# Edges of a graph network kernel laid on 128 partitions of 416 columns instead of 125 of 425

## The chip, the cores and the metric

The kernel runs on one core of one Trainium2 chip. The metric is device time in microseconds (us), the median of 16 runs. All numbers of the profile below come from one profiled execution on that core.

## The reference

A stack of four graph layers on 3,125 nodes of 256 features and 53,125 directed edges (25,000 edges both ways and one loop per node, sorted by destination `dst`). Each layer takes `h = relu(layernorm(x))` and adds its result to `x`.

```python
edge_index = jnp.stack([src, dst])
h = relu(layernorm(x)); x = x + L0(h, edge_index, edge_attr_64, ...)   # MLP message per edge, segment_sum over dst, MLP, layernorm
h = relu(layernorm(x)); x = x + L1(h, edge_index, edge_type_64, ...)   # attention, 4 heads, softmax per dst node
h = relu(layernorm(x)); x = x + L2(h, edge_attr_64, ..., edge_index)   # here dst = edge_index[0], src = edge_index[1]: sums over the SOURCE list
h = relu(layernorm(x)); x = x + L3(h, edge_index, ...)                 # attention, 1 head, then LSTM gates
```

Layer L2 reads the same edge list the other way round: it sums over what L0, L1 and L3 call the source. Its edges must therefore be sorted by source. `edge_attr_64` has 64 floats per edge.

## The kernel before, in words

Nodes are handled in 25 blocks of 128 (`NB`, `P`). Layers L0, L1 and L3 work by slots: the nodes are sorted by degree, and slot s of a block gathers the s-th neighbour of each of its 128 nodes by an indirect DMA (`gather`, line 154). L2 works by tiles: every block of 128 source nodes has 18 tiles of 128 edge records (the last block 8), 440 tiles in all.

`prelude` (line 243) sorts. It loads `dst`, `src`, `type` and the list `nxt_i` (each edge's next `dst`) as tiles of 125 partitions x 425 columns (`EP`, `EC`, lines 253 to 269): `dst_i` and the features `xh` on SyncE's queue (SP), the others on ScalarE's. It counts degrees by one-hot matmuls in two chunks of columns (`counted`, line 325: 153 VectorE comparisons and one matmul per column), ranks the nodes, and writes L0's table for the source nodes to DRAM (`table`, line 353). Between these the statistics of the layer norm are taken (`stats`, line 341). By running sums over 25 block masks (`scans`, line 461) it finds for each edge the row `row2` of the source-sorted record table `ss` in DRAM (line 555). Rows of `ss` that get no edge must read as empty: 40 DMAs fill the whole table from `sfill` before (line 304).

`by_slots` (line 561) then runs L0, L1, L2, L3. A record of `ss` is 66 floats: 64 attributes, the destination and the source's place in its block. The records are written during L0 and L1, column after column, by `scatter_src` (line 597): `loaded` (line 585) brings `CH = 5` columns of attributes of all 125 partitions into one of two buffers `rec` by a DMA on SP, `filled` (line 591) adds the two other fields by two VectorE copies, and five indirect DMAs (`scatter`, line 157) each write one column, 125 rows of 264 bytes. In L0's main loop each of 226 pairs of slots issues two gathers `gt` and, from the 19th on, one scatter. After the loop comes a drain: a hand-made clock (`Clock`, line 164) finishes the node updates, with two scatters per tick. In L1 the rest is spread over the groups of four slots, and 8 columns come at the end (line 1115).

GpSimd (POOL) issues all indirect DMAs, in the order in which they are written (`queued`, line 139). On SP and VectorE a scheduler sets the order of the instructions: it moves `loaded` and `filled` ahead of the place where they are written. An instruction of SP that waits holds up all behind it.

If a count of the input does not fit the planned slots and tiles, `flag` sends the program to another, slower path (`by_blocks`), which does not run here.

Of the kernel before, what the change touches and what calls it, by code (L numbers as in the profile page):

```python
# [9 lines left out]
F32 = mybir.dt.float32  # L10
I32 = mybir.dt.int32
BF = mybir.dt.bfloat16
AF = mybir.ActivationFunctionType
ALU = mybir.AluOpType
# [4 lines left out]
P = 128  # L19
N = 3125  # L20
NB = 25
NP = NB * P
LAST = N - (NB - 1) * P
E = 53125
EP, EC = 125, 425
# [5 lines left out]
NT = 440  # L31
# [3 lines left out]
SREC = 66  # L35
# [12 lines left out]
TILES = (18,) * (NB - 1) + (8,)  # L48
TM = TILES[0]
FR = mybir.dt.float32r  # L50
assert sum(TILES) == NT
XH = 516
# [4 lines left out]
def flat(ap, n):  # L57

    return bass.AP(tensor=ap.tensor, offset=ap.offset, ap=[[n, 1], [1, n]])


class Kit:


    last = [None, None]
# [158 lines left out]
class Lists:  # L224


    def __init__(self, pool):
        self.nid_i = pool.tile([P, NB], I32, name="nid_i")
        self.nid3_i = pool.tile([P, NB], I32, name="nid3_i")
        self.off_i = pool.tile([P, NB], I32, name="off_i")  # L230
        self.deg = pool.tile([P, NB], F32, name="deg")
        self.has = pool.tile([P, NB], F32, name="has")
        self.st = pool.tile([P, NB, SM, 2], I32, name="st")
        self.pen = pool.tile([P, NB, SM], F32, name="pen")
        self.srcb = pool.tile([P, NB, 2, HM], I32, name="srcb")
        self.ai = pool.tile([P, 2, NB], I32, name="ai")
        self.row2 = pool.tile([EP, EC], I32, name="row2")
        self.dst_e = pool.tile([EP, EC], F32, name="dst_e")
        self.srcl_e = pool.tile([EP, EC], F32, name="srcl_e")
# [3 lines left out]
def prelude(ctx, tc, a, a_d, nodes_d, ss, st_d, flag, t):  # L243
# [9 lines left out]
    dst_i = c.tile([EP, EC], I32, name="dst_i")  # L253
    nc.sync.dma_start(dst_i, a["dst"].rearrange("(p c) -> p c", c=EC))
# [5 lines left out]
    e_src = c.tile([EP, EC], I32, name="e_src")  # L260
    nc.scalar.dma_start(e_src, a["src"].rearrange("(p c) -> p c", c=EC))
    e_typ = c.tile([EP, EC], I32, name="e_typ")
    nc.scalar.dma_start(e_typ, a["edge_type_64"].rearrange("(p c) -> p c", c=EC))
    nxt_i = c.tile([EP, EC], I32, name="nxt_i")
    nc.gpsimd.memset(nxt_i, N)
    for p0, p1, w in ((0, EP - 1, EC), (EP - 1, EP, EC - 1)):
        nc.scalar.dma_start(nxt_i[p0:p1, 0:w],
                            bass.AP(tensor=a["dst"].tensor, offset=a["dst"].offset + p0 * EC + 1,
                                    ap=[[EC, p1 - p0], [1, w]]))
# [6 lines left out]
    sfill = c.tile([P, 11, SREC], F32, name="sfill")  # L276
# [12 lines left out]
    nc.gpsimd.memset(cap[:, NB - 1:NB], float(P * TILES[NB - 1]))  # L289
    none = c.tile([1, 512], F32, name="none")  # L290
# [13 lines left out]
    for i in range(40):  # L304
        nc.sync.dma_start(ss[i * 11 * P:(i + 1) * 11 * P, :].rearrange("(p r) c -> p (r c)", p=P),
                          sfill.rearrange("p r c -> p (r c)"))

    both_e = c.tile([EP, EC, 2], I32, name="both_e")
    nc.gpsimd.tensor_copy(both_e[:, :, 0], e_src)
    nc.gpsimd.tensor_copy(both_e[:, :, 1], e_typ)  # L310
    nc.scalar.dma_start(st_d.rearrange("(p c) -> p c", c=2 * EC), both_e.rearrange("p c i -> p (c i)"))


    lo_i = wk.tile([EP, EC], I32, name="lo_i", tag="edge", bufs=4)
    nc.vector.tensor_scalar(lo_i, dst_i, 127, None, op0=ALU.bitwise_and)
    lo = c.tile([EP, EC], BF, name="lo")
    nc.vector.tensor_copy(lo, lo_i)
    hi_i = wk.tile([EP, EC], I32, name="hi_i", tag="edge", bufs=4)
    nc.vector.tensor_scalar(hi_i, dst_i, 7, None, op0=ALU.logical_shift_right)
    hi = c.tile([EP, EC], BF, name="hi")  # L320
    nc.vector.tensor_copy(hi, hi_i)
    pdeg = ps.tile([P, NB], F32, name="pdeg")
    CW = 214

    def counted(hp, c0, c1):
        w = c1 - c0
        ol = hp.tile([EP, P, CW], BF, name="ol")
        oh = hp.tile([EP, NB, CW], BF, name="oh")
        for v in range(P):
            nc.vector.tensor_scalar(ol[:, v, 0:w], lo[:, c0:c1], float(v), None, op0=ALU.is_equal)  # L330
        for v in range(NB):
            nc.vector.tensor_scalar(oh[:, v, 0:w], hi[:, c0:c1], float(v), None, op0=ALU.is_equal)
        for i in range(w):
            nc.tensor.matmul(pdeg, ol[:, :, i], oh[:, :, i], start=(c0 + i == 0), stop=(c0 + i == EC - 1))
# [33 lines left out]
    with tc.tile_pool(name="ph", bufs=1) as hp:  # L368
        counted(hp, 0, CW)
        stats()  # L370
        table(0, 5)
        counted(hp, CW, EC)
# [73 lines left out]
    sl_i = wk.tile([EP, EC], I32, name="sl_i", tag="edge", bufs=4)  # L446
    nc.vector.tensor_scalar(sl_i, e_src, 127, None, op0=ALU.bitwise_and)
    nc.vector.tensor_copy(t.srcl_e, sl_i)
    hs_i = wk.tile([EP, EC], I32, name="hs_i", tag="edge", bufs=4)
    nc.vector.tensor_scalar(hs_i, e_src, 7, None, op0=ALU.logical_shift_right)  # L450
    hs = c.tile([EP, EC], BF, name="hs")
    nc.vector.tensor_copy(hs, hs_i)
    eq = op.tile([EP, NB, EC], BF, name="eq")
# [3 lines left out]
    zero = ps.tile([EP, EC], F32, name="zero")  # L457
    nc.vector.memset(zero, 0.0)
    cum = op.tile([EP, NB, EC], F32, name="cum")
# [8 lines left out]
    tots = c.tile([EP, NB], F32, name="tots")  # L468
    nc.vector.tensor_copy(tots, cum[:, :, EC - 1])
    pc3 = ps.tile([P, 4, NB], F32, name="pc3")  # L470
    pc2, pv = pc3[:, 0:2, :], pc3[0:1, 2, :]
    nc.tensor.matmul(pc2[:EP, 0, :], k.tri[:EP, :EP], tots, start=True, stop=True)
    nc.tensor.matmul(pc2[:, 1, :], k.ones[:EP, :], tots, start=True, stop=True)
    viol = wk.tile([EP, EC], F32, name="viol", tag="edge", bufs=4)
    nc.vector.tensor_tensor(viol, dst_i, nxt_i, ALU.is_gt)
    v1 = c.tile([EP, 1], F32, name="v1")
# [5 lines left out]
    nc.vector.tensor_tensor(over, pc2[:, 1, :], cap, ALU.is_gt)  # L482
    v3 = c.tile([P, 1], F32, name="v3")
    nc.vector.tensor_reduce(v3, over, AX.X, ALU.add)
    nc.tensor.matmul(pv[:, 0:1], v1, k.ones[:EP, 0:1], start=True, stop=False)
# [5 lines left out]
    bases = c.tile([EP, NB], F32, name="bases")  # L491
    nc.vector.tensor_scalar(bases, pc2[:EP, 0, :], -1.0, None, op0=ALU.add)
# [4 lines left out]
    for b in range(NB - 1, -1, -1):  # L497
        k.gather(t.st[:, b, 0:SLOTS[b], :].rearrange("p s i -> p (s i)"), flat(st_d, 2 * E), t.off_i[:, b:b + 1], axis=1)
# [46 lines left out]
    pos_i = wk.tile([EP, EC], I32, name="pos_i", tag="edge", bufs=4)  # L545
    nc.vector.tensor_copy(pos_i, cum[:, 0])
    pa_i = wk.tile([EP, EC], I32, name="pa_i", tag="edge", bufs=4)
    nc.vector.tensor_scalar(pa_i, pos_i, 127, None, op0=ALU.bitwise_and)
    pj_i = wk.tile([EP, EC], I32, name="pj_i", tag="edge", bufs=4)
    nc.vector.tensor_scalar(pj_i, pos_i, 7, None, op0=ALU.logical_shift_right)  # L550
    step = wk.tile([EP, EC], F32, name="step", tag="edge", bufs=4)
# [3 lines left out]
    nc.vector.scalar_tensor_tensor(t.row2, hs, float(P * TM), step, op0=ALU.mult, op1=ALU.add)  # L555
    nc.vector.tensor_scalar(t.dst_e, dst_i, float(KVQ), None, op0=ALU.mult)
# [3 lines left out]
def by_slots(ctx, tc, a, out, a_d, nodes_d, ss, t):  # L560
# [19 lines left out]
    attr = a["edge_attr_64"].rearrange("(p c) k -> p c k", c=EC)  # L580
    CH = 5
    recs = ctx.enter_context(tc.tile_pool(name="s_recs", bufs=2))
    done = [0]

    def loaded(c):

        rec = recs.tile([EP, CH, SREC], F32, name="rec")
        nc.sync.dma_start(rec[:, :, 0:64], attr[:, c:c + CH, :])
        return rec

    def filled(c, rec):
        nc.vector.tensor_copy(rec[:, :, 64], dst_e[:, c:c + CH])  # L592
        nc.vector.tensor_copy(rec[:, :, 65], srcl_e[:, c:c + CH])

    rec_of = {}

    def scatter_src(n):

        for _ in range(n):
            c = done[0]  # L600
            if c == EC:
                return
            c0 = c - c % CH
            if c == 0:
                rec_of[0] = loaded(0)
                filled(0, rec_of[0])
            if c % CH == 1 and c0 + CH < EC:
                rec_of[c0 + CH] = loaded(c0 + CH)
            if c % CH == 3 and c0 + CH < EC:
                filled(c0 + CH, rec_of[c0 + CH])  # L610
            k.scatter(ss, row2[:, c:c + 1], rec_of[c0][:, c % CH, :], "src_records")
            done[0] += 1
# [340 lines left out]
    with tc.tile_pool(name="s_e1", bufs=2) as wk, tc.tile_pool(name="s_e1w", bufs=1) as w, \  # L953
# [161 lines left out]
        left, shares, share = EC - 8 - done[0], sum(-(-c // U) for c in SLOTS), 0  # L1115
# [16 lines left out]
        scatter_src(EC)  # L1132
# [1206 lines left out]
def kernel(tc: tile.TileContext, a: dict, out: bass.AP):  # L2339
    nc = tc.nc  # L2340
    a_d = nc.dram_tensor("s_l0_src", [NP + 1, 512], F32, kind="Internal").ap()
    nodes_d = nc.dram_tensor("s_nodes", [NP, XH], F32, kind="Internal").ap()
    ss = nc.dram_tensor("s_src_records", [NT * P, SREC], F32, kind="Internal").ap()
    st_d = nc.dram_tensor("s_src_type", [2 * E], I32, kind="Internal").ap()
    with tc.tile_pool(name="flags", bufs=1) as flags:
        flag = flags.tile([1, 1], I32, name="flag")
        with tc.tile_pool(name="keep", bufs=1) as keep:
            t = Lists(keep)
            prelude(tc, a, a_d, nodes_d, ss, st_d, flag, t)
            _, v = nc.values_load_multi_w_load_instructions(  # L2350
                flag, engines=[ET.PE, ET.DVE, ET.Activation, ET.Pool, ET.SP], min_val=0, max_val=1,
                skip_runtime_bounds_check_because="a comparison's result")
            with tc.If(v[0] == 1):
                by_slots(tc, a, out, a_d, nodes_d, ss, t)
        with tc.If(v[0] == 0):
            by_blocks(tc, a, out)
# [31 lines left out]
```

## Time and profile before

| | |
|---|---|
| median of 16 runs (lowest, highest) | 3809.69 us (3803.84, 3820.55) |
| the profiled execution's own time | 3817.74 us |
| its span, first to last instruction | 3815.9 us |
| granted TensorE clock, mean | 0.775 |
| busy: PE, DVE, ACT, POOL | 2406.7, 2390.8, 1092.8, 2483.7 us |
| DMA | 595.89 MB, 156 GB/s |

PE is TensorE's matmuls, DVE is VectorE, ACT ScalarE, POOL GpSimd. The stages in the span: prelude 0 to 237 us, L0's main loop from 275.5 (its first sum) to 1256 (its last gather), the drain to 1419.7 (L1's first gather), L1 to about 2290, L2 to 3100, L3 to the end. In a timeline a row has the start, the duration, the engine, the line, the operation, out<-in, and in brackets the idle time before it and what ended it.

### The profile page before, as it was taken

How to read it: one execution, taken by the hardware profiler on the slowest of the kernel's cores; microseconds unless marked ns; L12 is line 12 of the kernel's file. 1: busy time of each engine (PE TensorE's matmuls, PEld its weight loads, DVE VectorE, ACT ScalarE, POOL GpSimd, SP SyncE). 2: the span in 40 equal slices, each digit the busy share in tenths (PEclk: the TensorE clock that was granted, in tenths of full speed). 3: DMA queues.
4: the chain of work that ended last, by engine and by line, in shares of the span. 5: the costliest groups of instructions: out<-in, count | busy, mean ns of one | idle time of the engine just before them, and what ended most of it. 6: DMA issues, size and time to landing. Idle time of an engine off the chain costs nothing. (4 is left out here: it accounts for less than half of the span.)

```text
span 3815.9 us, 32547 instructions
## 1 busy us (share of the span) xinstructions
PE 2406.7 (63%) x9174; PEld 1481.9 (39%) x9174; DVE 2390.8 (63%) x4836; ACT 1092.8 (29%) x2292; POOL 2483.7 (65%) x2497
## 2 busy tenths in 40 slices
PE   5827878788777544676766755998989731112123
PEld 3313434344343223454544543666666520001011
DVE  5646567576666315786877774898988924444444
ACT  1112122122211002222222222666766521112122
POOL 3447677777777775766667553667766436666664
PEclk9858889999988755777777677899999965555556
DMA  6346465666656336666666555566666443333332
GB/s 223 127 125 172 132 182 162 171 183 169 179 167 171 81 96 179 188 190 188 190 188 196 152 157 171 184 202 207 204 205 194 130 125 100 90 97 99 96 102 73
DMA packets 295839, 595.89 MB, mean 156 GB/s; under 512 B 113501, under 2 KB 154508, under 8 KB 295650
## 3 DMA queue, kind: packets, MB, share of 16 engines
q0 software_dynamic: 163616, 472.86, 42.7%
q1 hardware_dynamic: 131512, 119.79, 10.5%
q8 instruction: 76, 1.25, 0.1%
q10 hardware_dynamic: 522, 1.06, 0.1%
q14 instruction: 113, 0.93, 0.1%
HBM read 510.85 MB, written 82.21 MB: 155 GB/s over the span
## 5 line engine op out<-in xcount | busy, mean ns | idle before, releaser
L154 POOL DMA_INDIRECT kv<-s_l_rows,dst x440 | 457.2, 1039 | 218.1 <-issue 72.2
L158 POOL DMA_INDIRECT s_src_records<-rec,row x425 | 512.0, 1205 | 131.7 <-issue 122.0
L924 PE MATMUL ph<-wm,st 128*128 128x512 f32 x904 | 474.2, 652 | 129.0 <-DVE acc L943 65.3
L154 POOL DMA_INDIRECT gt<-s_l_src,srcb x452 | 433.8, 960 | 179.4 <-issue 108.5
L154 POOL DMA_INDIRECT kv<-s_l_kv,st x439 | 420.1, 957 | 174.3 <-issue 106.7
L154 POOL DMA_INDIRECT xg<-s_l_rows,src x439 | 415.8, 947 | 133.8 <-issue 133.8
L1034 PE MATMUL acc<-kv,ident 128*128 128x256 f32 x878 | 302.1, 501 | 126.0 <-DVE kv L1030 125.7
L134 PE MATMUL pt<-ident,hb 128*128 128x128 f32 x50 | 17.0, 442 | 549.8 <-ACT hb L1438 549.8
L938 DVE TENSOR_TENSOR ph<-gt,ph 128x1024 f32<-128x1024 f32 x226 | 276.8, 1225 | 113.5 <-PE ph L924 102.0
L924 PEld LDWEIGHTS ph<-wm,st 128*128 128x128 f32 x904 | 177.6, 207 | 332.7 <-issue 288.1
L1034 PEld LDWEIGHTS acc<-kv,ident 128*128 128x128 f32 x878 | 207.7, 248 | 192.8 <-DVE kv L1030 151.6
L990 PE MATMUL pk<-rel,toh 64*128 64x64 f32 x878 | 161.3, 339 | 154.2 <-DVE mk L992 101.6
L1289 PE MATMUL pg<-kv,oh 128*128 128x256 f32 x880 | 251.0, 411 | 3.7 <-DVE kv L1286 3.4
L943 DVE SCALAR_TENSOR_TENSOR acc<-ph,acc 128x1024 f32<-128x1024 f32 x201 | 244.8, 1218 | 3.0
L985 ACT ACTIVATE toh<-tb,negp 64x512 f32<-64x512 f32 (+3 forms) x119 | 81.8, 688 | 559.3 <-PE pk L990 498.3
L134 PEld LDWEIGHTS pt<-ident,hb 128*128 128x128 f32 x50 | 7.1, 201 | 578.8 <-ACT hb L1438 578.8
L1474 DVE TENSOR_SCALAR sc<-xg,own 128x4 f32<-128x4 f32 (+3 forms) x119 | 32.1, 269 | 314.7 <-DMA xg<-s_l_rows,src 307.5
L592 DVE COPY rec<-dst_e 125x5 f32<-125x5 f32 x85 | 16.2, 190 | 338.0 <-DMA s_src_records<-rec,row 312.4
L990 PEld LDWEIGHTS pk<-rel,toh 64*128 64x128 f32 x878 | 144.4, 246 | 199.8 <-issue 134.6
L1431 DVE SCALAR_TENSOR_TENSOR acc<-xg,sc,acc 128x256 f32<-128x256 f32 x439 | 212.6, 489 | 6.9
L1244 PE MATMUL pk<-we,eat 64*128 64x256 f32 x880 | 163.3, 444 | 46.6 <-DVE mk L1250 44.8
L1250 DVE TENSOR_TENSOR mk<-kv,pk 128x512 f32<-128x512 f32 x220 | 149.3, 679 | 49.1 <-DMA kv<-s_l_rows,dst 42.1
(373 smaller groups left out, 5427.5 us busy)
## 6 DMA issues: line engine op xcount, KB each, us to landing
s_src_records<-sfill SPq DMA_DIRECT2D x40, 363.0 KB
srec<-s_src_records SPq DMA_DIRECT2D x24, 594.0 KB
rec<-in_edge_attr_dram SPq DMA_DIRECT2D x85, 156.2 KB
tb<-s_slot_types SPq DMA_DIRECT2D x101, 128.0 KB
gt<-s_l_src,srcb POOLq DMA_INDIRECT x452, 3.7
kv<-s_l_rows,dst POOLq DMA_INDIRECT x440, 3.8
kv<-s_l_kv,st POOLq DMA_INDIRECT x439, 3.9
xg<-s_l_rows,src POOLq DMA_INDIRECT x439, 2.8
```

The costliest lines, as they stand in the source:

```text
L154: self.queued(lambda: self.nc.gpsimd.indirect_dma_start(out=to, out_offset=None, in_=table, in_offset=bass.IndirectOffsetOnAxis(ap=index, ...
L158: st = self.queued(lambda: self.nc.gpsimd.indirect_dma_start(out=table, out_offset=bass.IndirectOffsetOnAxis(ap=index, axis=0), in_=rows, ...
L924: nc.tensor.matmul(ph[:, h, :], stat[h][:, s % 4, :], ms[b][h], start=True, stop=True)
L938: nc.vector.tensor_add(ph, gt, ph)
L943: nc.vector.scalar_tensor_tensor(accs[b], ph, 0.0, accs[b], op0=ALU.max, op1=ALU.add)
L985: nc.scalar.activation(to, tb[:, 0:n * P], AF.Abs, bias=negp[:64])
L990: nc.tensor.matmul(pk[:, q, :], toh[:, q, :], rel, start=True, stop=True)
L1034: nc.tensor.matmul(acc, ident, v[:, q, :], start=(s0 + q == 0), stop=(s0 + q == C - 1))
L1244: nc.tensor.matmul(pk[:, i, :], eat[i * 64:(i + 1) * 64, q, :], we[i * 64:(i + 1) * 64, :], start=True, stop=True)
L1250: nc.vector.tensor_add(mk, o.kv[j // 2][:, :, 0:D], pk)
L1289: nc.tensor.matmul(pg, oh[:, j % T6 + i, :], v[:, i, :], start=(j + i == 0), stop=(j + i == n - 1))
L1431: nc.vector.scalar_tensor_tensor(acc, xgs[q // U3][:, q % U3, 0:D], s[:, q:q + 1], acc, op0=ALU.mult, op1=ALU.add)
```

## The change

The edges lie on 128 partitions of `ECW = 416` columns. The last partition has only `EL = 53125 - 127*416 = 293` edges. The places without an edge get a destination and a source past the nodes, so that no count sees them, and a row behind the table (`past`), which is 128 rows longer for that. Every load of an edge list is now two DMAs, 127 partitions and the last one. `rec` is a ring of three buffers of `CH = 4` columns, cleared once, and loads are written one chunk further ahead. Only the last three tiles of each block are filled by `sfill`, and `flag` also checks that every block reaches them (`low`). `counted` takes chunks of 208 columns instead of 214 and 211.

```diff
+ECW = 416
+EL = E - (P - 1) * ECW
+FULL = (15,) * (NB - 1) + (5,)
...
+    def edges(engine, to, of):
+        engine.dma_start(to[0:P - 1, :], of[0:(P - 1) * ECW].rearrange("(p c) -> p c", c=ECW))
+        engine.dma_start(to[P - 1:P, 0:EL], of[(P - 1) * ECW:E].rearrange("(p c) -> p c", p=1))
-    nc.sync.dma_start(dst_i, a["dst"].rearrange("(p c) -> p c", c=EC))
+    nc.gpsimd.memset(dst_i, 32 * P)
+    edges(nc.sync, dst_i, a["dst"])
...
-    nc.scalar.dma_start(e_src, a["src"].rearrange("(p c) -> p c", c=EC))
+    nc.gpsimd.memset(e_src, 32 * P)
+    edges(nc.scalar, e_src, a["src"])
...
+    past = c.tile([1, ECW - EL], I32, name="past")
+    nc.gpsimd.iota(past, pattern=[[1, ECW - EL]], base=NT * P, channel_multiplier=0)
-    sfill = c.tile([P, 11, SREC], F32, name="sfill")
+    sfill = c.tile([P, 3, SREC], F32, name="sfill")
...
-    for i in range(40):
-        nc.sync.dma_start(ss[i * 11 * P:(i + 1) * 11 * P, :]..., sfill...)
+    for b0, b1_ in ((0, 12), (12, NB - 1), (NB - 1, NB)):
+        nc.sync.dma_start(ss[r0:...].rearrange("(b p j) c -> p b (j c)", p=P, j=n)[:, :, FULL[b0] * SREC:n * SREC], sfill...)
...
-    CW = 214
+    CW = 208
...
     nc.vector.scalar_tensor_tensor(t.row2, hs, float(P * TM), step, op0=ALU.mult, op1=ALU.add)
+    nc.sync.dma_start(t.row2[P - 1:P, EL:ECW], past)
...
-    CH = 5
-    recs = ctx.enter_context(tc.tile_pool(name="s_recs", bufs=2))
+    CH = 4
+    recs = ctx.enter_context(tc.tile_pool(name="s_recs", bufs=1))
+    ring_ = [recs.tile([P, CH, SREC], F32, name=f"rec{i}") for i in range(3)]
+    for rec in ring_:
+        nc.gpsimd.memset(rec, 0.0)
     def loaded(c):
-        rec = recs.tile([EP, CH, SREC], F32, name="rec")
-        nc.sync.dma_start(rec[:, :, 0:64], attr[:, c:c + CH, :])
+        rec = ring_[c // CH % 3]
+        last = (P - 1) * ECW
+        nc.sync.dma_start(rec[0:P - 1, :, 0:64], attr[0:last, :].rearrange("(p c) k -> p c k", c=ECW)[:, c:c + CH, :])
+        w = min(CH, EL - c)
+        if w > 0:
+            nc.sync.dma_start(rec[P - 1:P, 0:w, 0:64], attr[last + c:last + c + w, :].rearrange("(p c) k -> p c k", p=1))
...
             if c == 0:
-                rec_of[0] = loaded(0)
-                filled(0, rec_of[0])
-            if c % CH == 1 and c0 + CH < EC:
-                rec_of[c0 + CH] = loaded(c0 + CH)
-            if c % CH == 3 and c0 + CH < EC:
-                filled(c0 + CH, rec_of[c0 + CH])
-            k.scatter(ss, row2[:, c:c + 1], rec_of[c0][:, c % CH, :], "src_records")
+                loaded(0)
+                filled(0)
+                loaded(CH)
+            if c % CH == 1 and c0 + CH < ECW:
+                filled(c0 + CH)
+            if c % CH == 3 and c0 + 2 * CH < ECW:
+                loaded(c0 + 2 * CH)
+            k.scatter(ss, row2[:, c:c + 1], ring_[c // CH % 3][:, c % CH, :], "src_records")
```

In the built order of instructions of the changed kernel SP issues the first part of `xh` ahead of `dst_i` (which waits for its memset); at the head of L0 it issues one `hp` (a block's node features, line 698), the loads of three chunks, and then the second `hp`. L0's main loop has 207 scatters and the drain 105, as before; L1 has 104 instead of 113. The instruction order of POOL is otherwise the same.

## The prediction, made before the changed kernel ran

> **What bounds the kernel now.** I read the busy times by stage first, then the timeline of POOL, then the DMA packets. Columns by stage: window, length, busy us of PE, PE's weight loads, DVE, ACT, POOL (instructions), granted clock, DMA share, GB/s.
>
> ```profile
> 275.50:1256.00 980.50, 796.23 (x2320) 399.30 (x2319) 626.86 (x880) 210.22 (x427) 737.38 (x713) 0.90 0.60 168
> 1256.00:1419.70 163.70, 81.41 (x192) 46.67 (x190) 41.62 (x139) 15.12 (x35) 129.62 (x112) 0.63 0.30 73
> 1419.70:2277.00 857.30, 566.02 (x2044) 409.46 (x2044) 613.02 (x958) 214.18 (x349) 559.09 (x557) 0.71 0.63 182
> ```
>
> The rows are L0's main loop, its drain and L1. POOL also spends about 0.30 us between two indirect DMAs, as the brackets of its timeline show. With it POOL is filled in the loop (737.4 + 713 x 0.30 = 951 of 980.5) and in the drain (129.6 + 34 = 163 of 163.7), and is not in L1 (559 + 167 = 726 of 857), where it shares the bound with DVE. L2 and L3 hold nothing that the change touches. Two kinds of scatter in the drain:
>
> ```profile
> 1326.77 1.18 POOL L158 DMA_INDIRECT s_src_records<-rec,row  x1 [0.30 <-issue]
> 1328.25 0.98 POOL L158 DMA_INDIRECT s_l_kv<-kv,nid_i  x1 [0.30 <-issue]
> 1329.54 1.19 POOL L158 DMA_INDIRECT s_src_records<-rec,row  x1 [0.30 <-issue]
> ```
>
> The record scatter has 125 rows of 264 bytes and takes 1.18 (mean over all 1.205, in the page's groups); the one between has 128 rows of 2 KB and takes 0.98. Row size is not the reason: gathers of 128 rows of 72 to 288 bytes (st, line 498) mostly take 0.94 too. The count of rows is.
>
> The count also sets over how many DMA engines a transfer is spread. ScalarE's queue on the page, then a window of the drain with exactly one load of rec:
>
> ```profile
> q10 hardware_dynamic: 522, 1.06, 0.1%
> ```
> ```profile
> q1 hardware_dynamic: 630, 0.16, 9.4%
> rec<-in_edge_attr_dram SPq DMA_DIRECT2D x1, 156.2 KB
> ```
>
> A load of rec has 5 x 125 = 625 pieces of 256 bytes; 630 means five more. The packet records show them as 4 bytes, one from each engine used: 5 for 125 rows. ScalarE's queue carried e_src, e_typ and both_e with 125 rows each, nxt_i with 124 and 1, and none with 1: 501 pieces, so 21 endings = 5 + 5 + 5 + 4 + 1 + 1. The 53-row rest of xh has one ending, and its pieces follow one another 45 ns apart. Loads of 128 rows have 16. So the number of engines is the largest up to 16 that divides the rows: 125 gives 5, 124 gives 4, 128 gives 16, the prime 53 gives 1. **The changed kernel loads 127 rows, a prime.** From the rows the bounds are 1 engine (as 53) and 16 (as 128); I take 1.
>
> The Trainium skill ("DMA: Bandwidth & Descriptors", section "Why a DMA increments its semaphore by 16 and not by 1") says the same against this change: such a copy uses the largest count up to 16 that divides the slowest dimension of both sides, and it names 127 partitions as a case of one engine. By this rule the sum is the one below, about +100 us; without it, by POOL's rows alone, it would be about -85.
>
> **The change, part by part**, against the profiled execution's 3817.7 us.
>
> *Scatters.* 416 instead of 425, and 128 rows: I take 0.98 for 1.205 (bounds 0.95 as the gathers, 1.205 unchanged). In the loop 207 x 0.225 = -47; it is POOL's, so it counts, less what other waits take back. In L1 nine scatters less, 9 x 1.505 = 13.5, and 95 x 0.225 = 21: -35 if all counts, 0 if DVE covers it; I take -15.
>
> *Prelude.* DVE starts when dst_i lands:
>
> ```profile
> 8.00 0.40 DVE L315 TENSOR_SCALAR lo_i<-dst_i 125x425 int32<-125x425 int32 x1 [6.44 <-DMA dst_i<-in_dst_dram]
> ```
>
> Its pieces (1,700 bytes, 72 ns each) came from 2.65 to 7.15 on five engines. Now 127 stand on one engine: 127 x 0.072 = 9.1 us, behind 48 pieces of xh (2.3 us), and beside ScalarE's lists, now 127 pieces each on the same engine. Alone it ends near 3 + 11.4 = 14.4; alternating piece by piece with the other queue (175 x 0.075 = 13.1) near 28. I take 23, so +15; fewer columns give back about 2 (25 scans at 0.93 us, 153 comparisons at 0.125, all 2% shorter). +13, bounds +5 to +20. The memsets ahead (0.45 us each) are in it. The last-row DMA of row2 makes SP wait for DVE's last sum (236.6) where it had issued w1b at 234.8: +2 (0 to 5). The 37 fills of sfill that go free SP until 72 us and 12 MB of DMA, but the first store behind them waited for its data at 73.2 anyway: 0.
>
> *Head of L0.* PE, SP before:
>
> ```profile
> 260.58 4.73 SPq L588 DMA_DIRECT2D rec<-in_edge_attr_dram  x2
> 265.35 2.22 SPq L804 DMA_DIRECT2D xh<-s_nodes  x2
> 269.95 3.43 SPq L698 DMA_DIRECT2D hp<-s_nodes  x2
> ```
> ```profile
> 272.65 0.38 PE L703 MATMUL pt<-ident,hp 128*128 128x128 f32 x2
> 272.87 0.27 PE L729 MATMUL pt<-ident,pair 128*128 128x128 f32 x1
> 273.48 0.70 PE L924 MATMUL ph<-wm,st 128*128 128x512 f32 x1 [0.34 <-ACT wm L715]
> ```
>
> PE transposes the second hp ahead of the first product. In the new order that hp stands behind three chunk loads. Per load 4 x 127 = 508 pieces on one engine; the first load before moved 125 per engine in 2.49 us, 19.9 ns a piece, so 3 x 508 x 19.9 = 30 us from about 265.6. hp lands near 297, PE wants it at 275: +22 (12 to 27). POOL is five pairs ahead and then stands, so all of it counts.
>
> *Loop.* A load takes 26.9 ns a piece there (mean of 41; 15.4 to 33.0): 508 x 26.9 = 13.7 us for four columns, in which POOL needs 4 x (2 x 1.25 + 1.28) + gathers of at, some 16 us. It fits, barely; other SP transfers (hp, xh, stores) stand behind it on that engine. I give back 22 of the 47: -25 (-47 if all is hidden, +54 if 33.0 ns and about 1.6 us of other transfers a chunk, 18.4 us, set the pace instead of 4 x 4.34 = 17.4).
>
> *Drain.* Nothing covers it here. POOL would do four columns in 4 x 1.28 = 5.1 us, but a load takes 508 x 20.2 (mean of 20 loads in the drain; 17.6 to 23.9) = 10.3 us. Of the 105 columns, those of about two chunks are there already; 24 loads x 10.3 = 246, and some 15 for the last scatters and node transfers: 261 against 163.7, so +95 (24 x 8.9 = 215 gives +56; 26.9 ns gives 343, +170). L1's first gather stands behind the last of these scatters.
>
> *L1.* One load in some 35 us is covered; tb has two buffers and PE's toh two more, about 16 us each. The weights at its head stand behind one or two loads: +10 (0 to 30). With the scatters -5 (-35 to +30).
>
> At nothing: the 19 more fills (0.17 + 0.16 us on DVE, which waits for scatters in the loop and drain anyway; 6 us if that goes), the one-row loads (4 pieces), the checks of low (two tiny DVE operations), the clearing of rec (three memsets near 0.3 us while SP loads weights).
>
> **Sum**: 13 + 2 + 22 - 25 + 95 - 5 = +102, so 3920 for an execution like the profiled one. That ran 8.05 above the median of the 16 runs, so **3911** as a median.
>
> **Rivals.**
> A, *faster: the loads do not bind.* If 127 rows spread over two engines or more, a load in the drain takes at most 508/2 x 20.2 = 5.1 us, which is POOL's own time; that is the deciding point. Then -47 in the loop, 105 x 0.225 = -24 in the drain, -15 in L1, 0 in the prelude: 3809.7 - 86 = 3724. For it: no row shows 127. Against: 53. Chance 0.10.
> B, *the scatter stays at 1.205*, because something other than the row count makes it. Only nine of them are saved. The loop loses its 47 us gain: -25 turns into +15 or so; L1 +10 more; the drain is the loads' either way: 3911 + 50 = 3961. Chance 0.10.
> C, *the loads bind the main loop as well.* 13.7 us of 16 leaves little, and a queue in order loses time at every wait of SP: +54 instead of -25, and the drain at 26.9 ns, +50 more: about 4040. Against: a load may be issued nine columns ahead, 35 us. Chance 0.17.
> D, *nothing*: gains and losses meet within 0.2% of the median, 7.6 us, about what a measurement of this kernel can tell from no change. Chance 0.04.
>
> **How the numbers follow.** The forecast, 3911, has 0.59. All its low bounds together give -8, near 3802; the high end takes in C: 4050. I leave out A and the far ends: 3800 to 4050. Its own range is 3850 to 3980. Faster: A and a sliver of the forecast's low end, 0.11; same 0.04; slower 0.85.
>
> **What would show it.** DVE's first sum on dst_i at 15 to 29 us instead of 8; PE idle some 20 us ahead of its first product of L0; the record scatters at 0.95 to 1.0 us; in the drain POOL idle ahead of record scatters, released by the loads of rec, and a length near 260; a window of one load with 508 pieces and one ending. I am wrong if the drain is shorter than 163 us (A), if the scatters take 1.2 (B), or if POOL waits for rec in the loop too (C).

## The result and the profile after

The changed kernel takes 3913.17 us (median of 8 runs, 3899.16 to 3919.28) against 3809.76 (43 runs): a ratio of 1.0263, 95% interval 1.025 to 1.0277. The profiled execution took 3912.32, its span is 3910.5. The prediction was 3911 in a range of 3800 to 4050. The total was right; several of its terms were not, and they made up for each other. That the total came within 2 us is luck.

The stages are cut at the same events in both traces: POOL's first gather `at`, DVE's first sum `ph`, POOL's last gather `gt`, its first gather `kv` of L1, its first of L2, and the end of the span. So L1 takes in some 80 us behind the 2277 at which its row in the prediction ends.

| stage | before | after | difference | predicted |
|---|---|---|---|---|
| prelude | 238.0 | 268.1 | +30.1 | +15 |
| head of L0 | 37.5 | 51.4 | +13.9 | +22 |
| L0's main loop | 979.8 | 939.7 | -40.1 | -25 |
| drain | 164.4 | 229.8 | +65.4 | +95 |
| L1 | 938.3 | 951.8 | +13.5 | -5 |
| L2 and L3 | 1458.0 | 1469.9 | +11.9 | 0 |

The groups of POOL on the page (instructions, busy us and mean ns, then the idle time before them and what ended most of it), before and after, show the shorter scatter and a new wait ahead of it:

```profile
L158 POOL DMA_INDIRECT s_src_records<-rec,row x425 | 512.0, 1205 | 131.7 <-issue 122.0
L162 POOL DMA_INDIRECT s_src_records<-rec,row x416 | 415.9, 1000 | 197.2 <-issue 114.2
```

1,000 ns stand where 1,205 stood, so rival B is out. But 197.2 us of idle time go ahead of the 416 scatters, and 83.0 of it ended with something other than POOL's own issue, where it was 9.7 before. The drain holds 76 of the 83; POOL's waits there (us in total, times, longest):

```profile
POOL s_src_records L162 <- DMA rec<-in_edge_attr_dram: 35.4, 12, 4.6
POOL s_src_records L162 <- DVE rec L623: 33.1, 10, 4.1
POOL s_src_records L162 <- issue: 26.5, 81, 2.1
POOL kv L158 <- DVE rel L987: 13.3, 1, 13.3
```

In the drain of before the scatters waited 32.1 in all, nearly all of it the 0.3 between any two instructions:

```profile
POOL s_src_records L158 <- issue: 30.6, 100, 0.5
```

The timeline of a piece of the new drain (start, duration; rows left out at the dots) shows one chunk after the other:

```profile
1325.89 7.58 SPq L618 DMA_DIRECT2D rec<-in_edge_attr_dram  x1
...
1333.65 0.29 SPq L615 DMA_DIRECT2D rec<-in_edge_attr_dram  x1
1333.98 7.29 SPq L618 DMA_DIRECT2D rec<-in_edge_attr_dram  x1
1336.47 0.17 DVE L622 COPY rec<-dst_e 128x4 f32<-128x4 f32 x1 [4.95 <-DMA s_src_records<-rec,row]
...
1337.32 0.96 POOL L162 DMA_INDIRECT s_src_records<-rec,row  x1 [3.73 <-DVE rec L623]
...
1341.94 0.23 SPq L615 DMA_DIRECT2D rec<-in_edge_attr_dram  x1
1342.21 7.75 SPq L618 DMA_DIRECT2D rec<-in_edge_attr_dram  x1
```

A chunk of four columns goes out every 8.2 us, while POOL needs 4 x 1.27 = 5.1 for it and waits the rest. L615 is the load of 127 rows; the small load of the last partition behind it (L618) stands 7 to 8 us on SP while the first is under way. The packet records give the load's 508 pieces as one unbroken row, 14.2 to 15.8 ns apart in the mean of a load. The last loads of the drain bring columns past 293 and have no small load behind them. Each of these has one ending, at 1447.55, 1455.07, 1463.18, 1470.66 and 1479.08, still 7.9 us apart, so the small load does not set the pace. The number of endings can also be counted on ScalarE's queue, in the page's list of queues (packets, MB):

```profile
q10 hardware_dynamic: 536, 1.07, 0.1%
```

Its DMAs now have three lists of 127 rows, three pieces for the last partition, 128 rows of `both_e` and one of `none`: 513 pieces. The other 23 are endings: 3 x (1 + 1) + 16 + 1. So 127 rows have one ending, as the rule from 125, 124 and 53 said.

The stages by their busy times (columns as in the prediction: length, PE, weight loads, DVE, ACT, POOL, clock, DMA share, GB/s), the loop, the drain and L1:

```profile
319.50:1259.50 940.00, 782.81 (x2321) 393.55 (x2321) 626.75 (x900) 211.10 (x427) 698.57 (x713) 0.93 0.60 175
1259.50:1489.00 229.50, 81.00 (x192) 46.45 (x190) 42.89 (x154) 14.88 (x35) 107.44 (x112) 0.59 0.19 53
1489.00:2440.60 951.60, 593.63 (x2170) 425.61 (x2171) 650.89 (x1052) 224.64 (x377) 551.15 (x568) 0.73 0.59 175
```

POOL lost 39 us of work in the loop and 22 in the drain. The loop became 40 shorter, and the drain 65 longer. In the head PE waits for `hp`, as foreseen, though for less:

```profile
315.14 0.66 PE L732 MATMUL pt<-ident,hp 128*128 128x128 f32 x2 [12.70 <-DMA hp<-s_nodes]
```

### The profile page after: what moved, and what is told of

Read it like the earlier page. It is cut to its first block, busy times and chain, and to the rows that moved or that the text cites. A ratio compares the mean times of both kernels' runs of the same rounds, so it can differ in the third digit from the quotient of the medians.

```text
span 3910.5 us, 32646 instructions
## 1 busy us (share of the span) xinstructions
PE 2380.7 (61%) x9165; PEld 1472.1 (38%) x9165; DVE 2389.7 (61%) x4876; ACT 1092.7 (28%) x2292; POOL 2400.9 (61%) x2497
## 5 line engine op out<-in xcount | busy, mean ns | idle before, releaser
L162 POOL DMA_INDIRECT s_src_records<-rec,row x416 | 415.9, 1000 | 197.2 <-issue 114.2
L622 DVE COPY rec<-dst_e 128x4 f32<-128x4 f32 x104 | 19.5, 190 | 372.9 <-DMA s_src_records<-rec,row 365.1
L1503 DVE TENSOR_SCALAR sc<-xg,own 128x4 f32<-128x4 f32 (+3 forms) x119 | 30.1, 253 | 319.2 <-DMA xg<-s_l_rows,src 316.8
```

Of the source, the lines that this page charges most:

```text
L162: st = self.queued(lambda: self.nc.gpsimd.indirect_dma_start(out=table, out_offset=bass.IndirectOffsetOnAxis(ap=index, axis=0), in_=rows, ...
```

## The experiments

Theory: the change has two causes, the row count of the scatters (a gain) and transfers of 127 rows on one engine (a loss). Rivals: the loss comes from the ring, the one-row loads or the fuller prelude; the gain comes from the layout. Four runs (the eight row counts, the first with loads of 113 + 12 rows, `b1` ahead of `xh`, the first in chunks of 8) fell on a chip on which the kernel before took 4195.58 instead of about 3800, and L0's loop moved 154 GB/s instead of 176 (chunks of 8 there, all loads spread here); of them only ratios within that chip, POOL's durations and the prelude are read.

| kernel | ratio to before, 95% | prelude | head | loop | drain | L1 |
|---|---|---|---|---|---|---|
| before | 1 | 238.0 | 37.5 | 979.8 | 164.4 | 938.3 |
| after | 1.0263 (1.025, 1.0277) | 268.1 | 51.4 | 939.7 | 229.8 | 951.8 |
| all loads spread | 0.9859 (0.9832, 0.9885) | 239.9 | 33.8 | 936.7 | 157.0 | 915.3 |
| loads of rec spread | 0.9932 (0.9906, 0.9958) | 268.9 | 34.4 | 937.1 | 157.0 | 908.1 |
| lists spread | 1.019 (1.0162, 1.0218) | 241.3 | 50.7 | 940.0 | 229.1 | 948.1 |
| before, scatters of 128 rows | 0.9827 (0.9795, 0.986) | 238.8 | 36.4 | 943.0 | 145.3 | 917.4 |
| before, loads of 113 + 12 | 1.0272 (1.0244, 1.03) | 236.1 | 45.3 | 983.2 | 230.0 | 957.6 |
| before, both | 1.014 (1.011, 1.0169) | 236.5 | 48.1 | 947.5 | 220.4 | 945.7 |
| all spread, again | 0.9854 (0.983, 0.9878) | 239.7 | 35.7 | 937.8 | 157.0 | 912.6 |
| all spread, chunks of 8 | 0.9772 (0.9743, 0.9801) | 241.1 | 33.7 | 934.4 | 165.6 | 874.4 |

L2 and L3, which no kernel here alters, took 1449 to 1470 in these executions. The 11.9 of the first table lies in that spread, and no cause is given for it.

**All loads spread.**

```diff
-        nc.sync.dma_start(rec[0:P - 1, :, 0:64], ...)
+        if c + CH <= EL:
+            nc.sync.dma_start(rec[:, :, 0:64], bass.AP(..., offset=attr.offset + c * 64,
+                                                       ap=[[ECW * 64, P], [64, CH], [1, 64]]))
+            return
+        for p0, p1 in ((0, 112), (112, P - 1)):
+            nc.sync.dma_start(rec[p0:p1, :, 0:64], ...)
```

The edge lists are cut at 112 in the same way.

> The changed kernel with every transfer of 127 rows cut so that it can use many engines: a chunk of rec is one load of 128 rows as long as the last partition is full (columns 0 to 288), behind that 112 + 15 rows; the lists dst, src, type and next are 112 + 15 + the last row. Nothing else differs. Theory (127 rows stand on one engine, and that alone is what the change costs): prelude back from 268 to about 240, head of L0 from 51 to about 37, drain from 230 to about 140 (the 164 of before less 105 scatters x 0.21), loop 930 to 940, L1 back under 938; in all 3720 to 3750, below the kernel before. Rival 1 (the loads are long for another reason: a ring of three, one-row loads, a fuller table): no stage moves, 3900 or more. Rival 2 (the loads are mended but POOL's shorter scatters are covered by DVE and PE): drain and prelude as before, loop not under 975, in all about 3800.

3744.57 (3740.48 to 3752.28), in the range of the theory. Its page has the same scatters, without the wait:

```profile
L162 POOL DMA_INDIRECT s_src_records<-rec,row x416 | 416.4, 1001 | 126.8 <-issue 118.3
```
```profile
q10 hardware_dynamic: 626, 1.07, 0.1%
```

The same 513 pieces have 113 endings: 3 x (16 + 15 + 1) + 16 + 1. So the transfers of 127 rows, with the small ones behind them, cost the change 4% (1.0263 - 0.9859, some 155 us), and without them it is 1.4% faster than the kernel before. The edit also takes the small load away for columns up to 291; that it is not the cause is seen in the drain above and in the kernels with 113 + 12 rows below. One figure was missed: the drain is 157, not 140. POOL's waits in it:

```profile
POOL s_src_records L162 <- issue: 27.1, 89, 0.3
POOL s_l_kv L162 <- DVE kv L890: 12.8, 1, 12.8
```

The loads are gone, and POOL now waits at the end for the last block of nodes. In before, POOL's last scatters were later than that block.

**Only the loads of rec, and only the lists.** Each takes one half of the edit above.

> The changed kernel with only the loads of rec cut as in the first of these kernels; the four edge lists of the prelude stay at 127 rows. Theory: drain, head and L1 as in the first kernel, the prelude stays near 268: about 28 above the first, 3750 to 3780. Rival (the long prelude and the long drain are one thing, such as a table that is filled late): both stay or both go.

> The changed kernel with only the four edge lists of the prelude cut to 112 + 15 rows and the last row; the loads of rec stay at 127 rows. Theory: the prelude falls from 268 to about 240, because DVE's first sum starts near 9 and PE's first product no longer waits for the row b1 behind xh; the rest stays, drain near 230: 3880 to 3890. Rival (the prelude is long because of its new work, that is the check, the column list and the POOL memsets ahead of the lists): it stays at 265 or more, 3910.

3773.04 and 3872.04. With the loads mended, drain, head and L1 fall and the prelude stays; with the lists mended, only the prelude falls. The two do not touch each other: 28.5 us lie between the first two kernels, 127 between the first and the third. (The third is 8 below its range; ranges were set from 3913, and the kernel before took 3799.58 beside it, ten less.)

**b1 ahead of xh.** The prelude rose by 30 where 15 were foreseen. DVE's first sum moved as predicted, from 8.00 to 22.41 (23 was taken):

```profile
22.41 0.38 DVE L335 TENSOR_SCALAR lo_i<-dst_i 128x416 int32<-128x416 int32 x1 [15.47 <-DMA dst_i<-in_dst_dram]
```

But SP's queue shows a second delay, and PE's timeline what hung on it (the first row is the load of `b1` in the kernel before):

```profile
18.22 0.73 SPq L94 DMA_DIRECT2D b<-in_L_gnn_eb_dram  x1
```
```profile
1.72 7.82 SPq L259 DMA_DIRECT2D dst_i<-in_dst_dram  x1
9.59 26.77 SPq L267 DMA_DIRECT2D xh<-in_x_dram  x3
36.47 0.35 SPq L269 DMA_DIRECT2D xh<-in_x_dram  x1
36.87 4.03 SPq L92 DMA_DIRECT2D w1a<-in_L_gnn_eW_dram  x1
47.28 0.25 SPq L98 DMA_DIRECT2D b<-in_L_gnn_eb_dram  x1
```
```profile
51.77 3.75 PE L381 MATMUL pa<-b,ones 1*128 1x512 f32 x4 [51.77 <-DMA b<-in_L_gnn_eb_dram]
55.44 16.84 PE L354 MATMUL pdeg<-oh,ol 128*128 128x25 bf16 x208
```

PE is built to take the product `pa` first, and that needs the row `b1`, which was issued at 18.22 in the kernel before and at 47.28 now. PE's sums of degrees stand behind it, and DVE waits for them, before and after:

```profile
DVE ol L330 <- PE pdeg L334: 10.1, 1, 10.1
DVE ol L350 <- PE pdeg L354: 22.9, 1, 22.9
```

The test moves two lines of the changed kernel:

```diff
     edges(nc.sync, dst_i, a["dst"])
...
-        nc.sync.dma_start(xh[:, b0:b0 + 6, 0:D], ...)
-    nc.sync.dma_start(xh[:LAST, NB - 1, 0:D], ...)
...
     w1a = k.load_w(c, a["L0_gnn_eW1"][0:D, :], "w1a")
     b1 = k.load_row(c, a["L0_gnn_eb1"], "b1", parts=1)
+        nc.sync.dma_start(xh[:, b0:b0 + 6, 0:D], ...)
+    nc.sync.dma_start(xh[:LAST, NB - 1, 0:D], ...)
```

> The changed kernel with the loads of w1a and the row b1 put ahead of the five loads of xh in SP's queue; the lists stay at 127 rows. It tells apart the two halves of the prelude's 30. Theory: about 15 of it is DVE's first sum, which starts when dst_i lands, and about 12 to 15 is PE's first product, which stands ahead of the sums of degrees on PE and needs b1, which is queued behind xh: the wait of DVE for PE's degrees falls from 22.9 to about 10, and the prelude from 268 to 253 to 258. Rival (the whole 30 comes from DVE's late start and from POOL's copies beside it): the prelude stays at 265 or more.

The prelude took 255.1, and DVE's wait is back at its old length, although the lists still stand on one engine:

```profile
DVE ol L349 <- PE pdeg L353: 10.1, 1, 10.1
```

So the 30 are about 17 from the late lists themselves and 13 from the row `b1` that comes late behind them; with the lists spread both are gone (241.3). (4317.07 in one run, on the slower chip; DVE's first sum started at 20.73 there.)

**The row counts of the scatter.** Eight counts in turn, by column, on the first kernel with the table filled whole:

```diff
-            k.scatter(ss, row2[:, c:c + 1], ring_[c // CH % 3][:, c % CH, :], "src_records")
+            if c % 8 == 0:
+                ... out=ss, ap=row2[0:128, c:c + 1], in_=ring_[c // CH % 3][0:128, c % CH, :]
+            elif c % 8 == 1:
+                ... out=ss, ap=row2[0:127, c:c + 1], in_=ring_[c // CH % 3][0:127, c % CH, :]
...
```

> The first kernel (all loads spread) with record scatters of eight row counts in turn, by column: 128, 127, 126, 125, 124, 120, 112 and 53 rows, each written on a line of its own; the edges of the partitions behind are left out of the table, so the layers behind L1 work on part of the edges. The table is filled whole again by 40 stores. Theory (POOL's own time of an indirect scatter goes by the largest count up to 16 that divides its rows): 128 and 112 rows (16) about 0.97 to 1.0, 120 rows (15) about the same, 126 rows (14) close above, 125 (5) 1.2, 124 (4) 1.2 to 1.3, 127 and 53 (1) 1.5 or more, although 53 rows are the fewest bytes. Rival (only a full set of 128 partitions is cheap): everything but 128 at 1.2. Rival 2 (the time goes by bytes): 53 rows the shortest. The full fill: prelude within 3 of the 239.9 of the first kernel if the stores are covered, 10 or more above if not.

Lines L644 to L665 hold 128, 127, 126, 125, 124, 120, 112 and 53 rows, in this order (POOL's duration in ns: least, median, most):

```profile
L644 POOL DMA_INDIRECT s_src_records<-rec,row x52: 989/1009/1017, 337.5 to 2576.5; - x52
L647 POOL DMA_INDIRECT s_src_records<-rec,row x52: 2543/2576/2849, 341.3 to 2577.8; - x52
L650 POOL DMA_INDIRECT s_src_records<-rec,row x52: 983/1012/1092, 347.3 to 2580.7; - x52
L653 POOL DMA_INDIRECT s_src_records<-rec,row x52: 1177/1216/1277, 351.2 to 2582.0; - x52
L656 POOL DMA_INDIRECT s_src_records<-rec,row x52: 1322/1355/1522, 355.2 to 2584.8; - x52
L659 POOL DMA_INDIRECT s_src_records<-rec,row x52: 978/1017/1226, 361.9 to 2586.4; - x52
L662 POOL DMA_INDIRECT s_src_records<-rec,row x52: 938/958/1154, 365.8 to 2587.7; - x52
L665 POOL DMA_INDIRECT s_src_records<-rec,row x52: 1550/1586/1811, 369.6 to 2589.0; - x52
```

Neither bytes nor "full or not" order these. The largest divisor up to 16 does: 16 (128, 112), 15 (120) and 14 (126) at about 1.0, 5 (125) at 1.22, 4 (124) at 1.36, 1 (127 and 53) at 2.58 and 1.59. A straight line through the two primes gives 0.88 plus 13.4 ns for each row of one engine. It makes 125 rows (25 an engine) 1.21, 124 (31) 1.29 and 128 (8) 0.98, so it holds within 6%. What the full fill costs stays open: the prelude took 252.0 in this single run, and 241.1 in the chunk-of-8 kernel of the same chip. By the expectation that says the 40 stores were not covered, but DVE's waits grew in several places, one of 14.1 us among them that the trace can't assign.

**Before, with scatters of 128 rows alone.**

```diff
-        self.row2 = pool.tile([EP, EC], I32, name="row2")
+        self.row2 = pool.tile([P, EC], I32, name="row2")
...
+    nc.gpsimd.iota(t.row2, pattern=[[1, EC]], base=NT * P - EP * EC, channel_multiplier=EC)
-        rec = recs.tile([EP, CH, SREC], F32, name="rec")
+        rec = ring_[c // CH % 2]
```

The two buffers have 128 partitions and are cleared once.

> The kernel before with one part of the change alone: its record scatters have 128 rows (partitions 125 to 127 hold zeros and go to 1,275 places behind the table), still 425 columns in chunks of 5, a ring of two, loads and lists of 125 rows, the full fill. Theory (the count of rows alone sets POOL's time of a scatter): 1.205 turns into 0.97 to 1.0, so the loop loses about 45, the drain 105 x 0.21 = 22 and L1 some: 3715 to 3745. Rival (the shorter scatter comes from the layout of 416 columns, the ring or the shorter loads): it stays at 1.2 and the time at 3810.

3736.24, with 1,001 ns for a scatter (425 of them) and loads, lists, columns and fill as before. The prelude is 238.8 with the 40 stores, and 239.9 with three in the kernel with all loads spread; the layouts differ, so what the removal is worth by itself is not shown. This is the change's gain by itself, and it needs no new layout: three idle partitions in the scatter suffice. The new layout with all its loads spread does no better (0.9859, with intervals that overlap).

**Before, with loads on one engine, and both together.**

```diff
-        nc.sync.dma_start(rec[:, :, 0:64], attr[:, c:c + CH, :])
+        nc.sync.dma_start(rec[0:113, :, 0:64], attr[0:113, c:c + CH, :])
+        nc.sync.dma_start(rec[113:EP, :, 0:64], attr[113:EP, c:c + CH, :])
```

> The kernel before with one thing alone: each load of rec, 125 rows over 5 engines, is cut into 113 rows (a prime) and 12. Theory: 113 x 5 = 565 pieces on one engine at 15.5 ns (the changed kernel's drain) are 8.8 a load, while POOL needs 5 x 1.49 = 7.4 for its five columns: the drain goes from 164 to 180 to 200, L1 rises by 10 to 35 because its loads of tb stand behind rec, the main loop stays within 5: a ratio of 1.007 to 1.018. Rival (the engine count of a load does not matter, the long drain has to do with the ring of three or with loads issued nine columns ahead): drain within 3 of 164, ratio 1.00.

4273.66, a ratio of 1.0195 (1.0139 to 1.0251) on the slower chip. The drain there was 229.0, beyond the range given, since the first piece of the next chunk came only some 2 us after the end of the last: one chunk in about 10.7, not 8.8. The same kernel again, and with the 128-row scatters:

> The kernel before with its loads of rec cut into 113 rows on one engine and 12 rows. Theory: drain from 164 to 200 to 230 (each chunk of five columns takes 8.8 for 565 pieces and about 2 until the next load is out, as in the run on the slower chip), L1 up by 10 to 35, loop within 5: a ratio of 1.015 to 1.025. Rival (the engine count does not matter): drain 164, ratio 1.00.

> The kernel before with both causes put in by hand: record scatters of 128 rows and loads of rec of 113 rows on one engine and 12 rows; lists of 125 rows, 425 columns, a ring of two, the full fill as before. Theory (the two causes alone make the change's result, but for its prelude): the loop gains as with 128-row scatters alone (943 to 950), the drain is as long as in the kernel beside it with 125-row scatters (215 to 235), because the loads set it and not POOL, L1 loses 15 to 35 against 917: 3840 to 3870, a ratio of 1.010 to 1.020. Rival (shorter scatters shorten the drain in any case, the gains add up): drain 20 below the kernel beside it, ratio under 1.005.

3901.77 and 3854.77. A prime row count put into the loads of the old kernel makes its drain 230.0, as long as the changed kernel's, with a ring of two, five columns and no one-row loads; those are not the cause. The drains of the two (length, busy times, clock, DMA share, GB/s):

```profile
1264.60:1494.60 230.00, 78.89 (x194) 44.91 (x192) 41.91 (x143) 15.12 (x35) 130.78 (x112) 0.61 0.24 58
```
```profile
1232.00:1452.40 220.40, 80.08 (x193) 44.51 (x191) 41.94 (x142) 15.12 (x35) 107.75 (x112) 0.60 0.21 60
```

POOL has 23 us less to do in the second, and the drain is only 10 shorter: the loads set its length. The loop keeps the gain (947.5 against 983.2). The second kernel lies in its ranges (loop, drain, L1 and total); the ratio of the first lies a little above its range, 1.0272.

**L1.** ACT's waits in L1 for the slot types `tb`, which SP loads in the same queue, in the kernel before, in the changed kernel and with all loads spread (second run):

```profile
ACT toh L985 <- DMA tb<-s_slot_types: 24.7, 6, 6.4
```
```profile
ACT toh L1014 <- DMA tb<-s_slot_types: 120.9, 16, 15.0
```
```profile
ACT toh L1020 <- DMA tb<-s_slot_types: 21.6, 7, 5.6
```

It was 107.0 in the one with loads of 113 + 12. One load in 35 us does not fill the queue, but `tb` stands behind it, ACT is late 16 times, and POOL's waits for PE's sums (`acc`) rise from 43.4 to 76.9.

**Chunks of 8.** One number, `CH = 8`, in the kernel with all loads spread; first on the slower chip, then beside the kernel with chunks of 4.

> The first kernel (all loads spread) in chunks of 8 columns instead of 4, ring of three: half as many loads and fills. In the first kernel the drain took 157 where POOL's 105 scatters and 5 stores are 140: POOL stood 12.8 for the last node block, whose steps on DVE stand behind fills that wait for scatters. Theory: with 13 fills instead of 26 in the drain, DVE waits less, the last block is done before the last scatter, and the drain falls to 140 to 146: 3725 to 3735, a ratio of 0.979 to 0.984. Rival (the last block is late because the fills come in later and each waits as long for its own scatter): the drain stays at 155 to 160 and the time at 3740 to 3750.

> The first kernel (all loads spread) once more, beside the next ones, since the chip of the last four took 10% longer for every kernel, the kernel before too. Theory: a ratio of 0.983 to 0.989 on a chip like the first; where the memory is slow, the scatters' gain is partly covered by other waits and the ratio is nearer to 1. Drain near 157, with POOL standing some 13 for the last node block.

> All loads spread, in chunks of 8 columns instead of 4. Theory (half as many fills let DVE finish the last node block before POOL's last scatter): drain 140 to 146 against 157 of the kernel beside it, ratio to that one 0.995 to 0.998. Rival (each fill now waits longer for its own scatters, so the block is as late): drain 155 or more, ratio to the kernel beside it 1.000 or above.

4220.41 on the slower chip (1.0078, 1.0048 to 1.0107); 3745.35 and 3711.04 on the other. On the slower chip the loop is 1073 with the short scatters, and 1072 in the kernel with loads of 113 + 12, whose scatters have 125 rows. POOL waits 148 us there for DVE's `ph`, where the same kernel waits 39 on the other chip, so the loop shows no gain from shorter scatters. 3711.04 is the best time of these kernels, but not for the reason given. The drain did not fall, it rose to 165.6:

```profile
POOL s_l_kv L162 <- DVE kv L890: 21.9, 2, 20.5
```

Half as many fills still left the last block of nodes late. In this drain DVE's fills waited 84.1 us for scatters in 12 waits, up to 9.2 each, against 95.4 in 26, up to 5.6, with chunks of 4. That fits the rival, by which each fill waits longer, though its price (a ratio of 1.000 or above) did not come: it is 0.991. That these waits are what delays the block is not shown; in the kernel before with scatters of 128 rows they come to 72.6, and POOL does not wait for the block. The gain is in L1, 874.4 for 912.6. There DVE's fills wait 19.6 us for scatters instead of 33.2 and the granted clock is 0.76 instead of 0.72; which of them is the cause was not tested.

## Why the prediction was right, step by step

**The mechanism** was right in both halves. 127 rows stand on one engine (23 endings), and 128-row scatters are short; each was put into the old kernel by itself and moved the stages that the prediction named. Rivals A, B and C are out: the drain is longer than 163, the scatter takes 1.000, and the loop lost 3 us to the loads (939.7 against 936.7 with the loads spread); D is out by the ratio, 1.0263. The rule of the Trainium skill that spoke against the change ("DMA: Bandwidth & Descriptors", section "Why a DMA increments its semaphore by 16 and not by 1") agrees with the endings counted here: 513 pieces made 536 packets with 127 rows, and 626 with 112 + 15.

**Prelude**, +15 predicted, +30 measured. The step that failed is the list of what waits for SP: it followed `dst_i` to DVE (22.41, foreseen 23) and costed the loads behind it at nothing. `b1` stood behind `xh`, and PE's sums behind `b1`: 13 more.

**Head**, +22 and +13.9. The size of a piece was too large, 19.9 ns from a load on five engines; the pieces of the three loads, 14.5 apart, came from 291.2 to 314.0, 23 us instead of 30.

**Loop**, -25 and -40. The 47 were 207 x 0.225; with the measured 1.000 they are 207 x 0.205 = 42. Of the 22 given back to the loads, about 3 were taken. A load written nine columns ahead was ready, as the reason against rival C said.

**Drain**, +95 and +65. Again the piece: 24 loads x 508 x 16 ns = 195, not 246. What stands beside them was 35 and not 15. The 73 between this drain and that with loads spread are the price of the one engine.

**L1**, -5 and +13.5. Both terms were too small: the scatters are worth 21 to 26 (917.4, 915.3 and 912.6 against 938.3), not 15; the loads cost 36 to 39 (951.8 against these last two), not 10, since they hold up `tb` all through the stage and not only the weights at its head. (The loads of 113 + 12 rows cost 19 and 28 there.)

**At nothing**: the checks, the memsets and the smaller fill come to 2 us together, by the prelude of the kernel with all loads spread (239.9 against 238.0); the fill by itself stays open. The small load of the last partition was not free for SP: it stands 7 to 8 us behind the big one. That a block of node steps is late next when the loads are mended was not seen; it is 13.

Three sums beside the forecast were off. The drain's low bound is 215 and the same 15, so +66 and not +56, and the range could have started some 10 higher; 343 is +179 and not +170; and rival C, whose drain is the same 343, added only 50 for it. The forecast itself does not use them.

The errors of the terms were +15, -8, -15, -30, +18 and +12: the sum came out 7 below the forecast by span because they cancelled, which no step of the prediction foresaw.

## What to carry to other kernels

Before a tile is laid on another number of partitions, take every transfer that it has and ask for the largest divisor up to 16 of its rows: 127 and 113 mean one engine, and cutting at 112 + 15 or adding idle rows to reach 128 cost nothing here that could be seen. A slow load that is hidden in a long loop is not hidden in the stage behind it, so price each stage by its own cover. And follow a delayed transfer through everything that stands behind it in its queue, and from there to what stands first on the engine that needs it.

## What had not been expected of the hardware

Over the eight row counts tried, an indirect scatter's time on POOL follows the same divisor as a plain transfer's spread: 2.58 us for 127 rows of 264 bytes, 1.01 for 126. A 256-byte piece came every 14 to 16 ns when one engine had a whole load (113 or 127 rows), where a load on five engines had taken 20 ns a piece and engine. And the three kernels that ran on both chips took 10 to 14% longer on one of them, with the loop at 154 GB/s; the kernel in chunks of 8 gained 2.3% on one chip and lost 0.8% on the other.
